# Graph-attention logits, masks and left sums on 32x32 tiles of TensorE, with the masks copied to all four row groups

## The chip, the cores and the metric

The kernel runs on one core of one Trainium2 chip. The metric is the device time of the whole program in microseconds (us); lower is better. The core has TensorE (PE), VectorE (DVE), ScalarE (ACT), GpSimd (POOL) and SyncE (SP, which here only issues transfers), and sixteen DMA engines that move data between its on-chip memory and DRAM.

## The reference

`x` has 4096 rows of 512 numbers, `adj` is a 4096 x 4096 matrix, mostly zero. Two layers follow each other, each on `h = relu(layernorm(x))` and each added to `x`:

```python
# layer 0: full attention with the adjacency added twice to the scores
a = q @ k.T / sqrt(512) + adj + adj
x = x + softmax(a) @ v

# layer 1: graph attention, 8 heads of 64
nX = standardized heads of h @ W            # per head: (nX - mean) / (std + eps), a_ln, b_ln
kg = at1 + at2.T                            # two numbers per node and head
kg = leaky_relu(kg, 0.2) * adj              # times the edge weight
mg = where(adj != 0, kg, -32768.0)
x  = x + elu(softmax(mg) @ nX + nX)
```

## The kernel before

**Layer 0** runs over 256 tiles: `ic`, eight chunks of 512 destinations, by `jt`, 32 blocks of 128 sources. A tile of `adj` is turned on VectorE so that sources lie on the partitions, scores are added to it (L734), the exponential is taken in place (L738), and the weighted values are summed on TensorE (L777). Along the way, `for_layer_1` makes two things out of each turned tile and stores them in DRAM: `ng`, bf16, zero on an edge and -2^60 elsewhere (L712, stored to `nT_d` by L715), and `gs`, the edge weight or a tiny number (L714, stored to `gT_d` by L716).

**Layer 1** begins with projections and ends with a software pipeline over 512 steps `STEPS[n] = (ic, hg, jt)`: eight chunks of 512 destinations, two groups of four heads, 32 blocks of 128 sources. The lines of a step:

- `load_adj(q)` loads four steps at once (JB = 4): `z2` (the sources' factors of the logits), the masks `nb` and `nx`, and the edge weights `g`. `nb` holds the masks on the partitions of their sources; `nx` holds the same rows with the two halves of 64 partitions exchanged. All go through SP's queue, two buffers each.
- `open_group(n, queue)` loads, once per group of 32 steps, `z1` (the destinations' factors), `u4`, and two six-row pieces of `z1_left`, whose other rows are zero.
- `sums(n)` makes the logits of four heads on TensorE: `z_product` (L1065), one matmul per head with six rows of the array at row group 32 x head, and then the masks: an identity times the mask, added to the logits (L1095), two heads at a time, four 64x64 tiles each. Two heads go to the left PSUM tile `l`, two to the right tiles `r`.
- `left_sums(n + 1)` (L1075) starts the next step's left tile with four 64x64 matmuls, and `left_relu` (L1081) takes 4 x relu of it on ScalarE in place; the logits are then added on top.
- `right_leaky` (L1113, VectorE) and `right_weigh` (L1119, GpSimd) finish the two right heads, `left_weigh` (L1122, VectorE) the two left ones. `exponent` (L1126, ScalarE) follows two steps later, `values` (L1134, TensorE, accumulated in `accs`) four steps later.

The program order on every engine is written out by hand and kept (`keep_in_program_order`, called `seq`); so are the places where loads are issued. In an iteration of the loop over `n` SP issues `load_adj(n // 4 + 1)` where `n` is a multiple of four, then what a group needs; TensorE does `sums(n)`, `left_sums(n + 1)` and `values(n - 4)`; `finish` and its tasks in `later` close a group. The projections' loop issues the first loads by `at_block(14, ...)`. Sources lie on the partitions as 4 column blocks of 32: P = 128, SB = 4, R = 32, HD = 64, GC = 512.

Of the kernel before, what the change touches and what calls it, by code (L numbers as in the profile page):

```python
# [11 lines left out]
BF16 = mybir.dt.bfloat16  # L12
# [6 lines left out]
P = 128  # L19
N = 4096  # L20
D = 512
NH = 8
HD = 64
NB = N // P
SB = 4
# [10 lines left out]
GC = 512  # L36
NI = N // GC
# [42 lines left out]
def fast_path(  # L80
# [18 lines left out]
    nc = tc.nc  # L99
    seq = tc.keep_in_program_order  # L100
# [3 lines left out]
    R = 32  # L104
# [10 lines left out]
    dram = ctx.enter_context(tc.tile_pool(name="dram", bufs=1, space=DRAM))  # L115
# [3 lines left out]
    ident_b = const.tile([P, P], BF16, name="ident_b")  # L119
# [25 lines left out]
    x1_d = dram.tile([NI, 2, P, SB, 2, P], F32, name="x1_d")  # L145

    gT_d = dram.tile([NB, P, N], F32, name="gT_d")
    nT_d = dram.tile([NB, P, N], BF16, name="nT_d")

# [1 line left out]
    z1_d = dram.tile([P, 2, N], BF16, name="z1_d")  # L153
# [172 lines left out]
    with tc.tile_pool(name="rows_in", bufs=2) as rows_in, tc.tile_pool(  # L326
        name="early", bufs=2
# [69 lines left out]
        with tc.tile_pool(name="proj_v", bufs=1) as pv, tc.tile_pool(  # L397
            name="proj_c", bufs=1
# [208 lines left out]
            for k in range(KC):  # L607
                pa = psum.tile([P, 512], F32, name="pa", tag="XZ"[k % 2], bufs=2)
                for c in range(SB):
                    seq(nc.tensor.matmul(  # L610
                        pa, turned["q"][:, c, ts(k, P)], turned["k"][:, c, :],
                        start=c == 0, stop=c == SB - 1,
# [71 lines left out]
        with tc.tile_pool(name="turns", bufs=6) as turns, tc.tile_pool(  # L684
            name="attn", bufs=2
# [22 lines left out]
            def for_layer_1(s):  # L708
                ic, jt = TILES[s]
                aT = turned[s] if s >= SB else firsts[s]  # L710
                ng = work.tile([P, GC], BF16, name="ng", tag="ng", bufs=2)
                seq(nc.vector.tensor_scalar(ng, aT, 0.0, NEG_BIG, ALU.is_equal, ALU.mult))  # L712
                gs = work.tile([P, GC], F32, name="gs", tag="gs", bufs=2)
                seq(nc.vector.scalar_tensor_tensor(gs, ng, G_MASKED / NEG_BIG, aT, ALU.mult, ALU.add))  # L714
                nc.sync.dma_start(out=nT_d[jt, :, ts(ic, GC)], in_=ng)  # L715
                nc.sync.dma_start(out=gT_d[jt, :, ts(ic, GC)], in_=gs)  # L716

            def product(out, s, name_a, name_b, start):
# [269 lines left out]
    with tc.tile_pool(name="ga_g", bufs=2) as adjs, tc.tile_pool(  # L988
        name="ga_in", bufs=2
    ) as inputs, tc.tile_pool(name="gat", bufs=1) as gat, tc.tile_pool(  # L990
        name="ga", bufs=2
# [7 lines left out]

        later = {}  # L1000

        z1_lefts = [gat.tile([P, GC], BF16, name=f"z1_left{k}") for k in range(2)]
        for z in z1_lefts:
            seq(nc.vector.memset(z, 0.0))

        def load_adj(q):
            ic, _, jt = STEPS[q * JB]
            z2 = inputs.tile([P, JB * P], BF16, name="z2", tag="z2", bufs=2)
            seq(nc.sync.dma_start(
                out=z2, in_=z2_d[:, STEPS[q * JB][1], jt * P : (jt + JB) * P]  # L1010
            ))
            ng = inputs.tile([P, JB, GC], BF16, name="nb", tag="nb", bufs=2)
            seq(nc.sync.dma_start(
                out=ng, in_=nT_d[jt : jt + JB, :, ts(ic, GC)].rearrange("t p i -> p t i")
            ))

            nx = inputs.tile([P, JB, GC], BF16, name="nx", tag="nx", bufs=2)
            for r in range(2):
                seq(nc.sync.dma_start(
                    out=nx[ts(r, HD)],  # L1020
                    in_=nT_d[jt : jt + JB, ts(1 - r, HD), ts(ic, GC)].rearrange("t p i -> p t i"),
                ))
            g = adjs.tile([P, JB, GC], F32, name="g", tag="g", bufs=2)
            seq(nc.sync.dma_start(
                out=g, in_=gT_d[jt : jt + JB, :, ts(ic, GC)].rearrange("t p i -> p t i")
            ))
            loads[q] = (g, (ng, nx), z2)

        def cols(ic, hg):
            rows = slice(ic * GC, (ic + 1) * GC)  # L1030
# [2 lines left out]
        def open_group(n, queue):  # L1033

            ic, hg, _ = STEPS[n]
            z1_left = z1_lefts[(2 * ic + hg) % 2]
            for first in (0, HD):
                rows = slice(first, first + 6)
                seq(queue.dma_start(out=z1_left[rows, :], in_=z1_d[rows, hg, ts(ic, GC)]))
            z1 = inputs.tile([P, GC], BF16, name="z1", tag="z1", bufs=2)  # L1040
            seq(queue.dma_start(out=z1, in_=z1_d[:, hg, ts(ic, GC)]))
            u4 = inputs.tile([P, 2, GC], F32, name="u4", tag="u4", bufs=2)
            groups[ic, hg] = {"z1": z1, "z1_left": z1_left, "u4": u4}
            load_u4(n, 0, queue)

        def load_u4(n, e, queue):
# [11 lines left out]

        lefts, rights = {}, {}

        def z_product(n, hh, out, start):

            ic, hg, jt = STEPS[n]
            rows = slice(32 * hh, 32 * hh + 6)
            seq(nc.tensor.matmul(  # L1065
                out, loads[n // JB][2][rows, ts(jt % JB, P)], groups[ic, hg]["z1"][rows, :],
                start=bool(start), stop=False, skip_group_check=not start,
            ))

        def left_sums(n):  # L1070

            lefts[n] = psum.tile([P, 2, GC], F32, name="l", tag="l", bufs=2)
            ic, hg, jt = STEPS[n]
            for r, c in ((0, 0), (1, 1), (0, 1), (1, 0)):
                seq(nc.tensor.matmul(  # L1075
                    lefts[n][ts(c, HD), r, :], loads[n // JB][2][ts(r, HD), jt % JB * P + c * HD :][:, :HD],
                    groups[ic, hg]["z1_left"][ts(r, HD), :], start=True, stop=True,
                ))

        def left_relu(n):  # L1080
            seq(nc.scalar.activation(lefts[n], lefts[n], AF.Relu, scale=4.0))  # L1081

        def sums(n):

            jt = STEPS[n][2]
            left = lefts[n]
            right = [psum.tile([P, GC], F32, name=f"r{e}", tag=f"r{e}", bufs=1) for e in range(2)]
            out = [left[:, 0, :], right[0], left[:, 1, :], right[1]]
            for hh in (1, 3, 0, 2):
                z_product(n, hh, out[hh], hh % 2)  # L1090
            masks = loads[n // JB][1]
            for first in (1, 0):
                for r, c in ((0, 0), (1, 1), (0, 1), (1, 0)):
                    rows = ts(r, HD)
                    seq(nc.tensor.matmul(  # L1095
                        out[first + 2 * r][ts(c, HD), :], ident_b[rows, rows],
                        masks[r != c][rows, jt % JB, :], start=False, stop=True,
                        skip_group_check=first == 0,
                    ))
            rights[n] = right  # L1100

        def both_heads(n):
# [361 lines left out]
        def at_block(r, f, *a):  # L1464
            at_blocks.setdefault(r, []).append(lambda: f(*a))
# [26 lines left out]
        at_block(0, rests[0])  # L1492
        at_block(12, first_group)
        at_block(14, load_adj, 0)
        for ic in range(2):
            load_normalized(ic)
        for r in range(-1, NB):
# [38 lines left out]
        for n in range(n_steps + 4):  # L1536

            q = n // JB + 1
            if n == n_steps:

                check_early()
                last_in.append(work.tile([P, HG, GC], F32, name="t", tag="t", bufs=6))
                for k, ap in enumerate((own_d[NI - 1, :, :, 1], x1_d[NI - 1, 1])):
                    seq(nc.sync.dma_start(
                        out=last_in[0][:, 2 * k : 2 * k + 2, :].rearrange("p f c -> p (f c)")
                        .rearrange("p (b d) -> p b d", b=SB),
                        in_=ap.rearrange("p b f d -> p b (f d)"),
                    ))
            if n % JB == 0 and q < n_steps // JB:
                load_adj(q)  # L1550
            if n + 10 < n_steps and STEPS[n + 10][2] == 0:
                open_group(n + 10, nc.sync)
            if n + 6 < n_steps and STEPS[n + 6][2] == 0:
                load_u4(n + 6, 1, nc.sync)
            if n < n_steps:
                sums(n)
            for f in left.pop(n, []):
                f()
            if n + 1 < n_steps:
                left_sums(n + 1)  # L1560
            if n < n_steps:
                right_leaky(n)
                right_weigh(n)
            if n + 1 < n_steps:
                left_relu(n + 1)
            done, ready = 0 <= n - 4 < n_steps, 0 <= n - 2 < n_steps
            if done and n < n_steps + 1:
                values(n - 4, 0)
            extra(n, "mid")
            if n < n_steps:  # L1570
                left_weigh(n)
            if done:
                if n < n_steps + 1:
                    values(n - 4, 1)
                if n % JB == 3:
                    loads.pop((n - 4) // JB)
            if n == n_steps + 3:
                for m, hf in ((n - 6, 0), (n - 5, 0), (n - 6, 1), (n - 5, 1)):
                    values(m, hf)
                for hf in range(2):  # L1580
                    values(n - 4, hf)
            if done and STEPS[n - 4][2] == NB - 1:
                if ready:
                    exponent(n - 2, slice(0, 2))
                finish(n, *STEPS[n - 4][:2])
                if ready:
                    exponent(n - 2, slice(2, 4))
            elif ready:
                exponent(n - 2)
            extra(n, "end")  # L1590
# [404 lines left out]
```

## Time and profile before

| what | value |
|---|---|
| median of 3 runs | 3541.22 us (3538.57 to 3542.74) |
| profiled execution: its own time | 3538.39 us |
| its span | 3536.6 us |
| mean granted TensorE clock | 0.996 |
| PE, DVE, ACT, POOL busy | 99%, 73%, 50%, 65% of the span |
| DMA | 779.07 MB, mean 220 GB/s |

The page divides the span into 40 slices and gives the busy share of each engine in each slice in tenths; layer 0 covers the first half and layer 1, whose loop begins near 1940 us, the second. The windows give the same by stretches of time. The chain of waits follows, from the last instruction back, what released each step. PEld is TensorE's loading of weights, which overlaps its matmuls; SPq is SP's queue of transfers.

### The profile page before, as it was taken

What the parts mean: (1) busy time and instruction counts of PE and PEld (TensorE: products, weight loads), DVE (VectorE), ACT (ScalarE), POOL (GpSimd) and SP (SyncE); (2) the same over time, 40 slices, a digit from 0 to 9 for tenths busy, and PEclk for the clock granted to TensorE, in tenths of its full rate; (3) what the DMA queues carried; (4) which work ended last, traced back from release to release, by engine and by line L of the source; (5) the groups of instructions that cost most, each with busy time, mean ns of one, the idle gap of its engine ahead of it and who ended that gap; (6) DMA issues with size and microseconds to landing.
All of it is one profiled execution on the core that took longest, in us unless ns stands there. A gap on an engine that the chain in (4) does not pass through costs nothing.

```text
span 3536.6 us, 59808 instructions
## 1 busy us (share of the span) xinstructions
PE 3492.0 (99%) x21898; PEld 2149.6 (61%) x21898; DVE 2574.3 (73%) x4262; ACT 1771.1 (50%) x1580; POOL 2285.6 (65%) x1863
## 2 busy tenths in 40 slices
PE   9999999999999999999999999999999999999998
PEld 7888888888888888888887223223222323232232
DVE  6765665656565666656567888888888888888887
ACT  2100111111111111111133999999999999999997
POOL 6754444444444444444567888788888888888886
PEclk9999999999999999999999999999999999999999
DMA  6688888888888888888768777787778877777885
GB/s 226 219 247 246 233 232 250 234 244 247 235 246 247 231 252 241 237 248 232 235 135 183 210 207 204 205 208 214 211 209 219 214 215 206 198 209 209 214 213 147
DMA packets 633550, 779.07 MB, mean 220 GB/s; under 512 B 78560, under 2 KB 461216, under 8 KB 624032
## 3 DMA queue, kind: packets, MB, share of 16 engines
q1 hardware_dynamic: 615680, 742.34, 73.5%
q0 software_dynamic: 16464, 31.98, 5.3%
q8 instruction: 174, 2.85, 0.3%
q10 hardware_dynamic: 1104, 0.85, 0.1%
q14 instruction: 128, 1.05, 0.1%
HBM read 592.97 MB, written 174.19 MB: 217 GB/s over the span
## 4 chain that ended last, share of the span: by engine, by line
PE 90%; DVE 7%; ACT 1%; DMA 1%; issue 1%; SPq 0%; DVEq 0%; ACTq 0%
PE accs L1134 25%; PE XZ L722 21%; PE M L777 20%; PE r L1095 4%; PE r L1065 4%; PE l L1075 3%; PE X L508 3%; PE l L1095 3%; PE Z L508 2%; DVE t L1122 2%; PE y L1327 1%; PE pt L1198 1%; DVE x L837 1%; DVE y L1211 1%; PE accs L1327 1%
## 5 line engine op out<-in xcount | busy, mean ns | idle before, releaser
L1119 POOL TENSOR_TENSOR t<-t,g 128x1024 f32<-128x1024 f32 x512 | 1225.6, 2406 | 268.9 <-DVE t L1113 233.3
L1134 PE MATMUL accs<-t,nX 128*64 128x512 f32 x4096 | 1003.0, 605 | 4.6 <-DVE ob L1188 4.6
L1126 ACT ACTIVATE t<-t 128x2048 f32<-128x2048 f32 (+1 forms) x527 | 976.5, 1853 | 0.2 <-POOL t L1119 0.2
L1113 DVE SCALAR_TENSOR_TENSOR t<-u,at2m,r 128x512 f32<-128x512 f32 x1024 | 719.3, 744 | 194.2 <-issue 152.0
L738 ACT ACTIVATE aT<-aT 128x512 f32<-128x512 f32 x256 | 161.2, 630 | 1387.3 <-DVE aT L734 1387.3
L734 DVE TENSOR_TENSOR aT<-aT,XZ 128x256 f32<-128x256 f32 x884 | 348.7, 418 | 575.1 <-PE XZ L722 570.8
L1122 DVE TENSOR_TENSOR t<-l,g 128x1024 f32<-128x1024 f32 x512 | 623.4, 1218 | 0.0
L1081 ACT ACTIVATE l<-l 128x1024 f32<-128x1024 f32 x512 | 516.3, 1008 | 117.5 <-PE l L1075 66.2
L1134 PEld LDWEIGHTS accs<-t,nX 128*64 128x64 f32 x4096 | 246.5, 136 | 461.9 <-issue 449.5
L722 PE MATMUL XZ<-qt,hS 128*128 128x256 f32 x2024 | 479.1, 379 | 1.0
L750 POOL TENSOR_TENSOR S<-aT 128x256 f32<-128x256 f32 x128 | 93.5, 731 | 506.9 <-ACT aT L738 506.9
L722 PEld LDWEIGHTS XZ<-qt,hS 128*128 128x128 f32 x2024 | 383.9, 190 | 55.9 <-DVE aT L734 4.0
L722 PE MATMUL XZ<-qt,hT 128*128 128x256 f32 x1520 | 369.5, 379 | 0.0
L762 POOL TENSOR_TENSOR total<-total,aT 128x256 f32<-128x256 f32 x360 | 323.0, 910 | 9.4
L722 PEld LDWEIGHTS XZ<-qt,hT 128*128 128x128 f32 x1520 | 288.8, 190 | 39.3
L1065 PEld LDWEIGHTS <-z 6*128 6x128 bf16 x2048 | 52.4, 91 | 422.2 <-DVE t L1113 353.8
L751 POOL TENSOR_TENSOR aT<-aT 128x256 f32<-128x256 f32 x128 | 93.6, 731 | 284.1 <-ACT aT L738 284.0
L777 PE MATMUL M<-tv,aT 128*128 128x256 f32 x1024 | 262.6, 379 | 0.0
L777 PE MATMUL M<-v,aT 128*128 128x256 f32 x1024 | 262.6, 379 | 0.0
L777 PE MATMUL M<-v,S 128*128 128x256 f32 x1024 | 242.5, 380 | 0.0
L714 DVE SCALAR_TENSOR_TENSOR gs<-ng,aT 128x512 f32<-128x512 bf16 x252 | 222.7, 884 | 8.7
L777 PEld LDWEIGHTS M<-v,aT 128*128 128x128 f32 x1024 | 194.6, 190 | 26.5
(267 smaller groups left out, 4552.4 us busy)
## 6 DMA issues: line engine op xcount, KB each, us to landing
g<-gT_d SPq DMA_DIRECT2D x128, 1024.0 KB
ag<-in_adj_dram SPq DMA_DIRECT2D x256, 256.0 KB
hS<-s_d SPq DMA_DIRECT2D x64, 1024.0 KB
gT_d<-gs SPq DMA_DIRECT2D x256, 256.0 KB
nb<-nT_d SPq DMA_DIRECT2D x128, 512.0 KB
nx<-nT_d SPq DMA_DIRECT2D x256, 256.0 KB
hT<-h_d SPq DMA_DIRECT2D x64, 768.0 KB
tv<-vt_d SPq DMA_DIRECT2D x128, 384.0 KB
```

The costliest lines, as they stand in the source:

```text
L714: seq(nc.vector.scalar_tensor_tensor(gs, ng, G_MASKED / NEG_BIG, aT, ALU.mult, ALU.add))
L722: seq(nc.tensor.matmul(out, a, b, start=start and k == 0, stop=k == 1, skip_group_check=not start,))
L734: seq(nc.vector.tensor_add(p, before, part))
L762: seq(nc.gpsimd.tensor_add(t, t, a))
L777: seq(nc.tensor.matmul(sums[ic][i][:, u, :], a[:, ts(u, P)], b, start=jt == 0 and u == 0, stop=jt == NB - 2, skip_group_check=u == 1,))
L1081: seq(nc.scalar.activation(lefts[n], lefts[n], AF.Relu, scale=4.0))
L1095: seq(nc.tensor.matmul(out[first + 2 * r][ts(c, HD), :], ident_b[rows, rows], masks[r != c][rows, jt % JB, :], start=False, stop=True, ski ...
L1113: seq(nc.vector.scalar_tensor_tensor(t[:, 2 + e, :], u4[:, e, :], at2m[:, jt, h : h + 1], right[e], ALU.max, ALU.add))
L1119: seq(nc.gpsimd.tensor_mul(t[:, 2:4, :], t[:, 2:4, :], both_heads(n)))
L1122: seq(nc.vector.tensor_mul(logits[n][:, 0:2, :], lefts.pop(n), both_heads(n)))
L1126: seq(nc.scalar.activation(t, t, AF.Exp))
L1134: seq(nc.tensor.matmul(accs[ts(e, HD), hf, :], nX[jt // SB][:, jt % SB, hg * HG + 2 * hf + e, :], t[:, hf + 2 * e, :], start=jt == 0, stop ...
```

## The change

`nT_d` gets a layout in which, for one tile, the four column blocks of 32 sources stand beside each other: 32 rows of 4 x 512. The store of `ng` is rearranged for it. `load_masks(n)` reads that block once per step and copies it to all four groups of 32 partitions, with a broadcast in front (four buffers, issued three steps ahead, ahead of `load_adj`); `nb` and `nx` and their loads are gone. So every row group of the array has all 128 sources' masks, 32 sources by 32 sources. `z_products` and the mask matmuls are written for 32x32 tiles, row group `hh` (the head) and column group `c` (the block of sources). `left_sums` uses `z_products` with `z1` itself, so `z1_left`, its loads and its memsets go.

```diff
--- before.py
+++ after.py
@@ -145,7 +145,7 @@
     x1_d = dram.tile([NI, 2, P, SB, 2, P], F32, name="x1_d")
 
     gT_d = dram.tile([NB, P, N], F32, name="gT_d")
-    nT_d = dram.tile([NB, P, N], BF16, name="nT_d")
+    nT_d = dram.tile([NB, NI, R, SB, GC], BF16, name="nT_d")
 
@@ -712,7 +712,7 @@
                 seq(nc.vector.tensor_scalar(ng, aT, 0.0, NEG_BIG, ALU.is_equal, ALU.mult))
                 gs = work.tile([P, GC], F32, name="gs", tag="gs", bufs=2)
                 seq(nc.vector.scalar_tensor_tensor(gs, ng, G_MASKED / NEG_BIG, aT, ALU.mult, ALU.add))
-                nc.sync.dma_start(out=nT_d[jt, :, ts(ic, GC)], in_=ng)
+                nc.sync.dma_start(out=nT_d[jt, ic].rearrange("p c i -> c p i"), in_=ng)
                 nc.sync.dma_start(out=gT_d[jt, :, ts(ic, GC)], in_=gs)
 
             def product(out, s, name_a, name_b, start):
@@ -999,32 +999,28 @@
 
         later = {}
 
-        z1_lefts = [gat.tile([P, GC], BF16, name=f"z1_left{k}") for k in range(2)]
-        for z in z1_lefts:
-            seq(nc.vector.memset(z, 0.0))
-
         def load_adj(q):
             ic, _, jt = STEPS[q * JB]
             z2 = inputs.tile([P, JB * P], BF16, name="z2", tag="z2", bufs=2)
             seq(nc.sync.dma_start(
                 out=z2, in_=z2_d[:, STEPS[q * JB][1], jt * P : (jt + JB) * P]
             ))
-            ng = inputs.tile([P, JB, GC], BF16, name="nb", tag="nb", bufs=2)
-            seq(nc.sync.dma_start(
-                out=ng, in_=nT_d[jt : jt + JB, :, ts(ic, GC)].rearrange("t p i -> p t i")
-            ))
-
-            nx = inputs.tile([P, JB, GC], BF16, name="nx", tag="nx", bufs=2)
-            for r in range(2):
-                seq(nc.sync.dma_start(
-                    out=nx[ts(r, HD)],
-                    in_=nT_d[jt : jt + JB, ts(1 - r, HD), ts(ic, GC)].rearrange("t p i -> p t i"),
-                ))
             g = adjs.tile([P, JB, GC], F32, name="g", tag="g", bufs=2)
             seq(nc.sync.dma_start(
                 out=g, in_=gT_d[jt : jt + JB, :, ts(ic, GC)].rearrange("t p i -> p t i")
             ))
-            loads[q] = (g, (ng, nx), z2)
+            loads[q] = (g, z2)
+
+        masks = {}
+
+        def load_masks(n):
+
+            ic, _, jt = STEPS[n]
+            masks[n] = inputs.tile([P, SB, GC], BF16, name="nb", tag="nb", bufs=4)
+            seq(nc.sync.dma_start(
+                out=masks[n].rearrange("p c i -> p (c i)"),
+                in_=nT_d[jt, ic].rearrange("p c i -> p (c i)").unsqueeze(0).to_broadcast([SB, R, SB * GC]),
+            ))
 
         def cols(ic, hg):
             rows = slice(ic * GC, (ic + 1) * GC)
@@ -1033,14 +1029,10 @@
         def open_group(n, queue):
 
             ic, hg, _ = STEPS[n]
-            z1_left = z1_lefts[(2 * ic + hg) % 2]
-            for first in (0, HD):
-                rows = slice(first, first + 6)
-                seq(queue.dma_start(out=z1_left[rows, :], in_=z1_d[rows, hg, ts(ic, GC)]))
             z1 = inputs.tile([P, GC], BF16, name="z1", tag="z1", bufs=2)
             seq(queue.dma_start(out=z1, in_=z1_d[:, hg, ts(ic, GC)]))
             u4 = inputs.tile([P, 2, GC], F32, name="u4", tag="u4", bufs=2)
-            groups[ic, hg] = {"z1": z1, "z1_left": z1_left, "u4": u4}
+            groups[ic, hg] = {"z1": z1, "u4": u4}
             load_u4(n, 0, queue)
 
         def load_u4(n, e, queue):
@@ -1058,45 +1050,42 @@
 
         lefts, rights = {}, {}
 
-        def z_product(n, hh, out, start):
+        def z_products(n, hh, out, **flags):
 
             ic, hg, jt = STEPS[n]
-            rows = slice(32 * hh, 32 * hh + 6)
-            seq(nc.tensor.matmul(
-                out, loads[n // JB][2][rows, ts(jt % JB, P)], groups[ic, hg]["z1"][rows, :],
-                start=bool(start), stop=False, skip_group_check=not start,
-            ))
+            rows = slice(R * hh, R * hh + 6)
+            for c in range(SB):
+                seq(nc.tensor.matmul(
+                    out[ts(c, R), :], loads[n // JB][1][rows, jt % JB * P + c * R :][:, :R],
+                    groups[ic, hg]["z1"][rows, :], **flags,
+                ))
 
         def left_sums(n):
 
             lefts[n] = psum.tile([P, 2, GC], F32, name="l", tag="l", bufs=2)
-            ic, hg, jt = STEPS[n]
-            for r, c in ((0, 0), (1, 1), (0, 1), (1, 0)):
-                seq(nc.tensor.matmul(
-                    lefts[n][ts(c, HD), r, :], loads[n // JB][2][ts(r, HD), jt % JB * P + c * HD :][:, :HD],
-                    groups[ic, hg]["z1_left"][ts(r, HD), :], start=True, stop=True,
-                ))
+            for r in range(2):
+                z_products(n, 2 * r, lefts[n][:, r, :], start=True, stop=True)
 
         def left_relu(n):
             seq(nc.scalar.activation(lefts[n], lefts[n], AF.Relu, scale=4.0))
 
         def sums(n):
 
-            jt = STEPS[n][2]
             left = lefts[n]
             right = [psum.tile([P, GC], F32, name=f"r{e}", tag=f"r{e}", bufs=1) for e in range(2)]
             out = [left[:, 0, :], right[0], left[:, 1, :], right[1]]
-            for hh in (1, 3, 0, 2):
-                z_product(n, hh, out[hh], hh % 2)
-            masks = loads[n // JB][1]
-            for first in (1, 0):
-                for r, c in ((0, 0), (1, 1), (0, 1), (1, 0)):
-                    rows = ts(r, HD)
+            order = (1, 3, 0, 2)
+            for hh in order:
+                right_one = hh % 2 == 1
+                z_products(n, hh, out[hh], start=right_one, stop=False, skip_group_check=not right_one)
+            for hh in order:
+                rows = ts(hh, R)
+                for c in range(SB):
                     seq(nc.tensor.matmul(
-                        out[first + 2 * r][ts(c, HD), :], ident_b[rows, rows],
-                        masks[r != c][rows, jt % JB, :], start=False, stop=True,
-                        skip_group_check=first == 0,
+                        out[hh][ts(c, R), :], ident_b[rows, rows], masks[n][rows, c, :],
+                        start=False, stop=True, skip_group_check=hh % 2 == 0,
                     ))
+            masks.pop(n)
             rights[n] = right
 
         def both_heads(n):
@@ -1492,6 +1481,8 @@
         at_block(0, rests[0])
         at_block(12, first_group)
         at_block(14, load_adj, 0)
+        for n in range(3):
+            at_block(14, load_masks, n)
         for ic in range(2):
             load_normalized(ic)
         for r in range(-1, NB):
@@ -1546,6 +1537,8 @@
                         .rearrange("p (b d) -> p b d", b=SB),
                         in_=ap.rearrange("p b f d -> p b (f d)"),
                     ))
+            if n + 3 < n_steps:
+                load_masks(n + 3)
             if n % JB == 0 and q < n_steps // JB:
                 load_adj(q)
             if n + 10 < n_steps and STEPS[n + 10][2] == 0:
```

## The prediction

> **What bounds the kernel now.** I read the page's busy times and slices first, then the windows of the two layers, then the chain of waits inside one layer-1 step, then the SP queue and the transfers, because the change touches matmuls and loads at once.
>
> ```profile
> PE 3492.0 (99%) x21898; PEld 2149.6 (61%) x21898; DVE 2574.3 (73%) x4262; ACT 1771.1 (50%) x1580; POOL 2285.6 (65%) x1863
> ...
> ACT  2100111111111111111133999999999999999997
> ...
> DMA  6688888888888888888768777787778877777885
> ```
>
> The second half (layer 1) has PE and ACT both at 9. The windows give shares:
>
> ```profile
> 335.00:2000.00 1665.00, 1651.75 (x7979) 1411.55 (x7981) 1047.67 (x2129) 301.80 (x455) 835.31 (x1034) 0.99 0.83 231
> 2040.00:3500.00 1460.00, 1447.41 (x11870) 435.00 (x11868) 1245.39 (x1559) 1355.93 (x995) 1198.14 (x550) 1.00 0.79 210
> ```
>
> Columns: window, length, busy PE, PEld, DVE, ACT, POOL, then clock, DMA share, GB/s. In layer 1 PE is busy 99%, ACT 1355.93/1460 = 93%, the sixteen DMA engines 79% on average. In layer 0 the DMA engines are at 83% beside a PE that never waits.
>
> The chain of waits through one step of layer 1 is TensorE alone:
>
> ```profile
> 2798.78 0.32 PE r L1065 x2
> 2799.11 0.01 PE l L1065 x2
> 2799.11 0.34 PE r L1095 x4
> 2799.45 0.22 PE l L1095 x4
> 2799.67 0.22 PE l L1075 x4
> 2799.89 1.87 PE accs L1134 x8
> 2801.75 0.32 PE r L1065 x2
> ```
>
> A step takes 2801.75 - 2798.78 = 2.97 us: 1.11 us of logits, masks and left sums, 1.87 us of values. So a step is PE's, ACT is next at 0.93 x 2.97 = 2.75 us, and loads hide. How four steps are loaded stands in the timeline of the SP queue:
>
> ```profile
> 2811.03 0.33 SPq L1009 DMA_DIRECT2D z<-z_d  x1
> 2811.57 0.36 SPq L1013 DMA_DIRECT2D nb<-nT_d  x1
> 2812.02 1.25 SPq L1019 DMA_DIRECT2D nx<-nT_d  x2
> 2815.43 0.36 SPq L1024 DMA_DIRECT2D g<-gT_d  x1
> ```
>
> The next four come 11.9 us later. And two windows show that equally busy DMA engines need not move equally much (last columns again: clock, share, GB/s):
>
> ```profile
> 2803.00:2805.00 2.00, 2.00 (x16) 0.41 (x12) 2.00 (x3) 2.00 (x2) 1.32 (x2) 1.00 0.98 192
> 2809.00:2810.50 1.50, 1.50 (x8) 0.29 (x4) 1.50 (x3) 1.50 (x2) 0.91 (x2) 1.00 1.06 356
> ```
>
> In the first mostly `nx` moves, in DMAs that write 64 partitions; in the second, rows for all 128. By the packet records a 1,024-byte row takes about 88 ns in the first and 46 ns in the second.
>
> **What the Trainium skill says.** "DMA: Bandwidth & Descriptors", section "Why a DMA increments its semaphore by 16 and not by 1": a DMA is split over the largest k up to 16 that divides the slowest dimension of both access patterns, and on SP's queue each of those k engines posts one +1. Its "Rules for kernel authors" add that a leading broadcast of c copies confines a DMA to at most c engines. The trace agrees with the rule: SP issued 2,232 DMAs, and its queue q1 has 35,392 four-byte packets, exactly 16 x 2,200 + 6 x 32; the 32 are the `z1_left` loads, which have six rows. "SBUF — State Buffer", section "Door 1: The DMA port swizzle": partitions 0-31 and 32-63 lie on the same eight of sixteen ports. The 88 ns against 46 agree. "TensorE: Matmul & The Clock Gate", Part 3: sixteen 32x32 tiles run together, starts some 4 ns apart. The trace shows it for four 64x64 tiles (3 to 4 ns apart); sixteen it doesn't show.
>
> **The change, part by part.**
>
> TensorE. Left sums go from 4 matmuls to 8, logits from 4 to 16, masks from 8 to 16: 16 become 40, with as many weight loads. If sixteen tiles overlap, the masks are one pack instead of two and save the 0.22 us of "l L1095"; logits and masks then use one tile size, which may save the 0.32 - 0.22 = 0.10 us that the logits take over a pack. 24 more starts at 4 ns cost 0.10 us. Net -0.2 us (bounds -0.3, and +1.1 if tiles of one row group went one after another: twice 0.88 and 0.44 against 1.11). -0.2 us is also all that ACT's 2.75 us lets through.
>
> The mask load. Its source is `unsqueeze(0).to_broadcast([SB, R, SB * GC])`: the slowest dimension is 4 (copies), the destination's is 128. By the rule k = 4: engine c carries the copy for partitions 32c to 32c+31, 32 rows of 4,096 bytes, every step. No row of before has such a packet on this queue; between the medians for 3,072 bytes (121 ns) and 8,192 bytes (309 ns) a straight line gives 158 ns, so 32 x 158 = 5.1 us per step on four engines (bounds 4.7, and 9.6 if each packet takes the 1.9-fold of the 64-partition rows). The same four also carry their sixteenth of the rest: `g`, 8 rows x 90 ns = 0.7; `z2`, 2 x 50 = 0.1; the accumulating transfers of POOL's queue, 9.2% of a 2.97 us step in the window 2400 to 3400, 0.27; `u4`, output, instruction fetches and semaphores about 0.1. That is 1.2 us. Against this, `nb` and `nx` go (1 MB per four steps over sixteen engines). I take 5.5 us for the masks, some packets meeting on a port, since engines drift: at 2812.0 one still brings `g` rows while others are in the next loads. Sum 5.5 + 1.2 = 6.7 us a step. Four mask buffers keep three transfers queued, so those engines never rest and their 6.7 us is the period; PE, ACT, DVE and POOL (2.97 us at most) hide beneath, with any gain or loss of TensorE below 3.7 us.
>
> SP's queue. Per four steps 6 DMAs instead of 5, at 0.33 to 0.36 us: 2.1 us of 27, free. load_masks(n+3) waits at the head for PE to finish the masks of step n-1; behind it stand `z2`, `g`, `u4` and the output. `g` follows up to four mask loads on the four rings and is needed four steps later; it lands with the last of them, so it adds its own 0.7 us, counted above. Two `z1_left` loads per group, two memsets and the first three mask loads (during the projections) lie off the path: 0.
>
> Layer 0. The store `nT_d[jt, ic].rearrange("p c i -> c p i")` also has a slowest dimension of 4. A tile of the loop takes (1785.3 - 241.7)/255 = 6.05 us between exponentials (L738); 0.83 of it is 5.0 us per engine. The store's 8 rows x 46 = 0.4 us become, on four engines, 32 x 46 to 32 x 88 = 1.5 to 2.8 us: 6.1 to 7.4 us against 6.05. PE loses 0 to 1.35 us per tile; waits at shared ports within the 0.83 ease when twelve engines are ahead, so I take 0.3 x 256 = 80 us (0 to 350; nothing here is on PE's path, so no gain).
>
> **Sum.** In the profiled execution (span 3536.6, its time 3538.4, 2.8 under the median of 3541.2) layer 1's loop runs from the first L1119 at 1941.2 to the last at 3513.9: 1572.7 us for 511 periods. The rest is 3538.4 - 1572.7 = 1965.7. After: 1965.7 + 80 + 512 x 6.7 (3430) = 5476; with the 2.8 us to the median 5480 us.
>
> **The rivals.**
>
> (a) Same confinement, ports shared throughout. Engines 0 and 1 walk partitions 0-31 and 32-63 in step, so every packet meets another on its port. For it: the 192 GB/s window. Against: a lag of four rows takes them apart. 9.6 + 1.2 = 10.8 us a step: 1966 + 150 + 5530 = 7650. In between lies everything from 5500 up.
>
> (b) Faster: the mask load spreads over sixteen engines, so that the four-fold copy is cheap. Then an engine has 8 x 158 ns = 1.3 us plus 1.2 us, 2.5 us in a 2.97 us step, and stays hidden; TensorE's -0.2 us shows: 3541 - 512 x 0.2 = 3440. It decides wherever the load falls below 2.75 us per step, which needs about ten engines or more. Against it: the count of 35,392, and the broadcast as the slowest dimension in the diff.
>
> (c) Sixteen engines, but tiles of a row group serialize: +1.1 us x 512 gives 4100, slower.
>
> That the change does not do what it says: it does load four row groups, but "broadcast" is the very thing that costs.
>
> **How the numbers follow.** Forecast 0.58, (a) with the stretch below it 0.34, (b) 0.05, (c) 0.03. Slower 0.94; faster 0.05; within 0.2% (about what a measurement of this kernel can tell from no change) 0.01. Forecast's low end: masks 4.7, others 1.1, layer 0 at 0: 5.8 x 512 + 1969 = 4940, rounded to 5050 because both lows at once are unlikely; the top is (a), 7650. That leaves out (b), (c) and a sliver of either end.
>
> **What would show it.** Right: a layer-1 step near 6.7 us (L1119 starts), PE at roughly half, waiting at the mask matmuls for `nb`; ACT near 40%; mean DMA share far below 0.79 in layer 1 while the time grows; packets of 4,096 bytes near 158 ns, about 260 ns or more for (a); k = 4 in the count of four-byte packets. The forecast is wrong if PE stays at 99%, or the share stays near 0.8: then the load was spread. Layer 0 is wrong if its loop keeps 6.05 us or exceeds 7.4.

## The result and the profile after

| | before | after |
|---|---|---|
| median | 3540.36 us (6 runs) | 5490.61 us (5482.04 to 5500.56, 6 runs) |
| ratio | 1 | 1.5513, 95% interval 1.5496 to 1.553 |
| span of the profiled execution | 3536.6 us | 5490.3 us |
| layer 0, from one exponential to the next (L738) | 6.05 us | 6.11 us |
| layer 1, mean step (first to last right weighing: L1119 before, L1108 after) | 3.08 us | 6.85 us |

The kernel is slower by 1950 us, nearly all of it in layer 1: its 511 steps took 3500.3 us in place of 1572.7. The loop starts 26.6 us later (1967.8 against 1941.2), of which layer 0 makes 14 us.

The page of the changed kernel, busy times and slices:

```profile
PE 4161.6 (76%) x34186; PEld 2238.2 (41%) x34186; DVE 2585.6 (47%) x4260; ACT 1778.1 (32%) x1580; POOL 2268.7 (41%) x1863
...
PE   9999999999999866665666666666666666666566
...
DMA  6788889888888654444444444444444444444443
GB/s 220 244 224 243 235 247 240 236 243 235 242 242 230 153 137 134 133 132 133 133 131 134 130 135 133 133 136 128 131 137 129 135 132 133 135 130 134 135 128 112
```

Read the DMA row against the time. In layer 1 the mean share of sixteen engines fell from 7 or 8 tenths to 4, and the bytes per second fell too, while the kernel grew longer. A mean of 0.4 looks like spare capacity; it is four engines without a pause and twelve mostly idle. The records of single packets show it: from 2100 to 5300 us four of the 4,096-byte packets that the mask load consists of are under way at once in 54% of the time, three or fewer in 40%, and five or six in 6% (records of successive packets can overlap). Packets of any kind are fewer than four at once in 1% of the time. The windows say the same (busy PE, PEld, DVE, ACT, POOL, then clock, share, GB/s):

```profile
335.00:2000.00 1665.00, 1620.58 (x7845) 1401.59 (x7843) 1019.95 (x2090) 263.57 (x424) 795.59 (x1016) 0.99 0.85 227
2100.00:5300.00 3200.00, 2031.05 (x22822) 510.95 (x22823) 1228.44 (x1530) 1337.08 (x976) 1164.73 (x536) 0.71 0.44 133
```

Four full engines of sixteen are 0.25. The rest of 0.44 is what the other loads take on the twelve others. The chain of waits through layer 1, which was TensorE alone, is now the mask load:

```profile
3953.96 23.50 DMA nb<-nT_d
3977.46 0.04 issue
3977.50 0.62 PE r L1084 x8
3978.13 0.03 PE l L1084 x8
3978.16 0.43 PE l L1058 x8
3978.59 1.17 PE accs L1123 x3
3979.76 24.55 DMA nb<-nT_d
```

One load takes 23 to 25 us from issue to the end. That is three and a half steps of 6.85 us: up to four loads stand in line for the same four engines. The engines' waits (engine, line, what it waited for: us in total, times, longest):

```profile
ACT l L1070 <- PE l L1058: 2024.8, 511, 9.2
...
PE r L1084 <- DMA nb<-nT_d: 1269.7, 422, 8.7
```

TensorE waits at the mask matmuls (L1084) for `nb`, and ScalarE, behind it in the order, for the next left sums.

The count of four-byte packets confirms the split. SP issued 2,328 DMAs, of which 768 have a slowest dimension of 4 (512 mask loads, 256 stores): 16 x 1,560 + 4 x 768 = 28,032, and the queue q1 has 28,032 such packets.

### The profile page after: what moved, and what is told of

Its sections match the earlier page's. It is cut to its first block, busy times and chain, and to the rows that moved or that the text cites. A ratio compares the mean times of both kernels' runs of the same rounds, so it can differ in the third digit from the quotient of the medians.

```text
span 5490.3 us, 84578 instructions
## 1 busy us (share of the span) xinstructions
PE 4161.6 (76%) x34186; PEld 2238.2 (41%) x34186; DVE 2585.6 (47%) x4260; ACT 1778.1 (32%) x1580; POOL 2268.7 (41%) x1863
## 4 chain that ended last, share of the span: by engine, by line
DMA 61%; PE 35%; DVE 2%; SPq 2%; issue 1%; ACT 0%; POOL 0%; DVEq 0%; ACTq 0%; POOLq 0%
DMA nb<-nT_d 54%; PE XZ L722 12%; PE M L777 11%; PE accs L1123 3%; DMA z<-z_d 3%; DMA tv<-vt_d 3%; PE X L508 2%; PE Z L508 2%; PE r L1084 1%; PE y L1316 1%; PE l L1058 1%; SPq L1020 1%; DMA gT_d<-gs 1%; PE accs L1316 1%; DVE aT L734 0%
## 5 line engine op out<-in xcount | busy, mean ns | idle before, releaser
L1108 POOL TENSOR_TENSOR t<-t,g 128x1024 f32<-128x1024 f32 x512 | 1206.3, 2356 | 2217.9 <-DVE t L1102 1902.5
L1123 PE MATMUL accs<-t,nX 128*64 128x512 f32 x4096 | 1545.7, 891 | 0.0
L1084 PE MATMUL r<-nb,ident_b 32*32 32x512 bf16 x4096 | 276.6, 514 | 1271.6 <-DMA nb<-nT_d 1269.7
L1084 PEld LDWEIGHTS <-ident_b 32*32 32x32 bf16 x8192 | 118.5, 93 | 1440.6 <-issue 1440.4
L1123 PEld LDWEIGHTS accs<-t,nX 128*64 128x64 f32 x4096 | 339.6, 188 | 762.5 <-issue 762.4
L738 ACT ACTIVATE aT<-aT 128x512 f32<-128x512 f32 x256 | 161.2, 630 | 1401.9 <-DVE aT L734 1401.9
L1058 PE MATMUL l<-z,z 6*32 6x512 bf16 x8192 | 527.1, 490 | 6.8 <-DMA z<-z_d 4.6
L1058 PEld LDWEIGHTS <-z 6*32 6x32 bf16 x12288 | 136.5, 91 | 690.7 <-issue 426.0
L1084 PE MATMUL l<-nb,ident_b 32*32 32x512 bf16 x4096 | 276.8, 516 | 0.0
```

Source lines behind the costliest of these rows:

```text
L1058: seq(nc.tensor.matmul(out[ts(c, R), :], loads[n // JB][1][rows, jt % JB * P + c * R :][:, :R], groups[ic, hg]["z1"][rows, :], **flags,))
L1084: seq(nc.tensor.matmul(out[hh][ts(c, R), :], ident_b[rows, rows], masks[n][rows, c, :], start=False, stop=True, skip_group_check=hh % 2 == ...
L1108: seq(nc.gpsimd.tensor_mul(t[:, 2:4, :], t[:, 2:4, :], both_heads(n)))
L1123: seq(nc.tensor.matmul(accs[ts(e, HD), hf, :], nX[jt // SB][:, jt % SB, hg * HG + 2 * hf + e, :], t[:, hf + 2 * e, :], start=jt == 0, stop ...
```

## The experiments

**Four loads in place of one broadcast.** Same bytes, same packets, same TensorE work; only the slowest dimension changes from 4 to 32.

```diff
-            seq(nc.sync.dma_start(
-                out=masks[n].rearrange("p c i -> p (c i)"),
-                in_=nT_d[jt, ic].rearrange("p c i -> p (c i)").unsqueeze(0).to_broadcast([SB, R, SB * GC]),
-            ))
+            for c in range(SB):
+                seq(nc.sync.dma_start(
+                    out=masks[n][ts(c, R)].rearrange("p c i -> p (c i)"),
+                    in_=nT_d[jt, ic].rearrange("p c i -> p (c i)"),
+                ))
```

> The changed kernel with each step's mask load as four loads of 32 rows, one per row group, in place of one load with the broadcast in front; bytes, packets and TensorE's work are the same. Theory (the broadcast's slowest dimension of 4 confines the load to four engines): each load now runs on sixteen engines, but its 32 partitions reach eight ports, so 524 KB at the 192 GB/s of the 64-partition loads of before take 2.7 us, plus 1.2 us for the rest: 3.9 us a step, about 3980 us in all, the four-byte packets up to 16 per load. Rival (twice the mask bytes are too many for the memory): the step stays at 6.85 us, about 5490 us. Rival (the 40 small matmuls at a lowered clock are the bound): also about 5490 us.

Measured: 3891.03 us, ratio to before 1.0992 (1.0974 to 1.101), a little better than I gave; a step takes 3.74 us, a 4,096-byte packet 259 ns in the mean (181 in the changed kernel). The queue has 58,752 four-byte packets, 16 x 1,560 + 4 x 256 + 16 x 2,048: each of the 2,048 loads ran on sixteen engines. The window of layer 1:

```profile
2100.00:3500.00 1400.00, 1216.32 (x18408) 369.34 (x18409) 986.24 (x1235) 1071.34 (x787) 946.02 (x437) 0.91 0.96 245
```

The share is 0.96: now all sixteen engines are full. Of the 1950 us, spreading the load over them brought back 1600 us. Both rivals (too many bytes, TensorE) are refuted as the main cause. That the remaining 350 us come from engines that meet at the eight ports of 32 partitions is argued from the packet time. The next run writes 128 partitions in one load.

**The same load from 128 different rows.**

```diff
+            first = ic // SB * SB
             seq(nc.sync.dma_start(
                 out=masks[n].rearrange("p c i -> p (c i)"),
-                in_=nT_d[jt, ic].rearrange("p c i -> p (c i)").unsqueeze(0).to_broadcast([SB, R, SB * GC]),
+                in_=nT_d[jt, first : first + SB].rearrange("a p c i -> (a p) (c i)"),
             ))
```

> The changed kernel with a mask load of the same size and packet length whose source is 128 different rows (four neighbouring chunks of destinations, so the masks are those of other destinations). Slowest dimension 128 on both sides: sixteen engines and all ports. Theory: masks 1.3 to 1.5 us plus 1.2 us per engine and step, hidden; what is left is TensorE's own gain or loss. I expect -0.2 us a step against before, about 3440 us (3400 to 3560). If 32x32 tiles of one row group went one after another it would be about 4100 us. Rival (mask bytes are too many): 5490 us.

Measured: 3579.03 us, ratio 1.0113 (1.0096 to 1.0129). The same bytes, with packets back at 159 ns in the median, now cost 38 us against before (82 us against the run without mask traffic below), so they are not too many. But my 3440 us were a miss, and so was the range from 3400 up to 3560. This run changes three things against the four loads: the partitions of one load, the rows that are read (128 different ones in place of 32 read four times) and the number of loads. So it does not show alone that the ports are the reason of the 350 us. The 64-partition `nx` loads of before speak for the ports: each reads different rows, and their packets were slow too. The window:

```profile
2040.00:3450.00 1410.00, 1314.09 (x22058) 426.17 (x22052) 1179.89 (x1477) 1273.42 (x944) 1133.29 (x521) 0.97 0.87 291
```

PE is busy 93% in place of 99%, the DMA share is 0.87 at 291 GB/s. Undisturbed steps take 2.8 us, the mean is 3.12 us. The run with kept masks and the one with a deeper queue show where the gain went.

**Two broadcasts of two.** The suspected cost doubled, the bytes kept.

```diff
-            seq(nc.sync.dma_start(
-                out=masks[n].rearrange("p c i -> p (c i)"),
-                in_=nT_d[jt, ic].rearrange("p c i -> p (c i)").unsqueeze(0).to_broadcast([SB, R, SB * GC]),
-            ))
+            for c in range(2):
+                seq(nc.sync.dma_start(
+                    out=masks[n][ts(c, HD)].rearrange("p c i -> p (c i)"),
+                    in_=nT_d[jt, ic].rearrange("p c i -> p (c i)").unsqueeze(0).to_broadcast([2, R, SB * GC]),
+                ))
```

> The changed kernel with each step's mask load as two loads, each a broadcast of two copies (64 partitions); same bytes and packets. Theory[...]: both loads fall on the same two engines, 64 packets x 162 to 182 ns = 10.4 to 11.6 us plus 1.2 us: 11.6 to 12.8 us a step, 7900 to 8540 us in all. Rival (each load takes its own pair of engines): four engines as before, near 5490 us. Rival (bytes or TensorE): 5490 us.

Measured: 7949.97 us (one run), 11.62 us a step, packets of 168 ns in the mean: 64 x 168 ns = 10.8 us, and 0.8 left over. The window of layer 1:

```profile
2100.00:3500.00 1400.00, 671.60 (x5873) 154.51 (x5873) 314.70 (x388) 346.24 (x255) 297.55 (x135) 0.60 0.24 78
```

The share halves to 0.24. Two loads of two copies do not take four engines between them: both fall on the same pair. The packet records agree: from 2100 to 3500 us two 4,096-byte packets are under way at once in 83% of the time, three in 4%, and never four. With steps of 11.62 us on two engines, 6.85 on four and 3.74 on sixteen, the cause of the main loss is settled.

**Layer 0's store, in two forms.** First as four stores of 32 rows, then in plain row order.

```diff
-                nc.sync.dma_start(out=nT_d[jt, ic].rearrange("p c i -> c p i"), in_=ng)
+                for c in range(SB):
+                    nc.sync.dma_start(out=nT_d[jt, ic][:, c, :], in_=ng[ts(c, R)])
```

> The changed kernel with layer 0's store of the masks as four stores of 32 rows (slowest dimension 32, sixteen engines) in place of one with a slowest dimension of 4. Theory: a tile of layer 0 goes from 6.11 back to 6.05 us, -14 us in all, about 5475 us; layer 1 keeps 6.85 us. Rival (four more transfers per tile on SP's queue cost as much as they save): layer 0 stays at 6.11 us or above.

Measured: 5487.29 us (one run), 6.10 us per tile of layer 0. Spreading the store over sixteen engines did not help: a miss.

```diff
-                nc.sync.dma_start(out=nT_d[jt, ic].rearrange("p c i -> c p i"), in_=ng)
+                nc.sync.dma_start(out=nT_d[jt, ic].rearrange("p c i -> (p c) i"), in_=ng)
```

> The changed kernel with layer 0's store of the masks in plain row order (128 rows on sixteen engines and all ports; the order of the sources in the masks is then not the one that layer 1 takes them for). If the rearranged store causes layer 0's 0.06 us more per tile, its tile goes from 6.11 to 6.05 us; if it stays at 6.11, the store is not the cause. Layer 1 keeps about 6.85 us a step; in all 5475 to 5490 us.

Measured: 5473.65 us (one run), 6.05 us per tile, as before. A tile takes 6.11 to 6.13 us in all six runs of this document that have the rearranged store in one piece, and 6.05 in the three with rows in plain order. So the rearranged store is the cause of layer 0's 14 us, in either form. The waits in layer 0 of the changed kernel, 335 to 1790 us,

```profile
PEld M L777 <- issue: 14.8, 26, 1.5
PE M L777 <- DMA tv<-vt_d: 5.4, 11, 1.1
```

and of this run

```profile
PEld M L777 <- issue: 0.6, 2, 0.5
```

show where the time goes: TensorE stands before the weighted values. 5.4 us of it are named as waits for `tv`, which arrives late. Why four stores of 32 rows delay it as much (eight ports, or four more transfers in front of `tv`) these runs do not tell.

**TensorE's part alone.** The masks of the first four steps are kept and used throughout.

```diff
-            masks[n] = inputs.tile([P, SB, GC], BF16, name="nb", tag="nb", bufs=4)
-            seq(nc.sync.dma_start(
...
+            if n < 4:
+                kept.append(inputs.tile([P, SB, GC], BF16, name=f"nb{n}", tag=f"nb{n}", bufs=1))
+                seq(nc.sync.dma_start(
...
+            masks[n] = kept[n % 4]
```

> The changed kernel with the masks of the first four steps kept and used in all steps (mask loads left out after these, so the masks are those of other tiles). TensorE's work is the same 40 small matmuls a step; no mask traffic in layer 1. Theory (TensorE's part alone saves 0.2 us a step, as its undisturbed steps of 2.77 to 2.80 us show in the run with 128 different rows, and that run's loss against before is bursts of transfers): mean step about 0.15 to 0.2 us under that of before (3.08 us from first to last L1119 there), 3440 to 3490 us in all. Rival (the 40 matmuls bring other waits, with POOL and ACT): 3540 us or above.

Measured: 3496.67 us, ratio 0.988 (0.9863 to 0.9896); mean step 2.94 us, 0.14 below before. The total is just above the 3490 I gave, because the loop starts 30 us later (1971.4 against 1941.2; about half of it is layer 0). The chain of waits of one step:

```profile
2801.81 0.34 PE r L1060 x8
2802.14 0.03 PE l L1060 x8
2802.17 0.19 PE r L1086 x8
2802.36 0.03 PE l L1086 x8
2802.39 0.35 PE l L1060 x8
2802.74 1.87 PE accs L1125 x8
2804.61 0.34 PE r L1060 x8
```

Logits, masks and left sums take 0.94 us in place of 1.11: sixteen mask matmuls pass in one pack of 0.22 us and start 2 to 5 ns apart. So sixteen 32x32 tiles do overlap, and the change's own idea works. Without any mask traffic it is worth 1.2%.

The left sums, the 0.35, took 0.22 before. VectorE holds them up:

```profile
2801.07 1.22 DVE L1113 TENSOR_TENSOR t<-l,g 128x1024 f32<-128x1024 f32 x1
...
2801.97 0.40 PE L1086 MATMUL r<-nb,ident_b 32*32 32x512 bf16 x8
...
2802.34 0.41 PE L1060 MATMUL l<-z,z 6*32 6x512 bf16 x8
```

`left_weigh` (L1113) reads the left tile of an earlier step and ends at 2802.29; the left sums, which need one of the two buffers, start 0.05 us later. From 2400 to 2800 us they start within 0.08 us of its end in 128 of 137 steps; in the kernel before, in 18 of 130. So of what TensorE saves, about 0.13 us a step is lost again to VectorE.

**Logits and left sums alone on 32x32 tiles**, masks as before.

```diff
-            seq(nc.tensor.matmul(
-                out, loads[n // JB][2][rows, ts(jt % JB, P)], groups[ic, hg]["z1"][rows, :],
...
+            for c in range(SB):
+                seq(nc.tensor.matmul(
+                    out[ts(c, R), :], loads[n // JB][2][rows, jt % JB * P + c * R :][:, :R],
...
+            for r in range(2):
+                z_products(n, 2 * r, lefts[n][:, r, :], start=True, stop=True)
```

> The kernel before with the logits and left sums alone on 32x32 tiles; masks, their loads and their 64x64 tiles as before. Theory: packs of matmuls stay as many as before (logits, two of masks, left sums), the switch from 32x32 to 64x64 tiles stays and one more comes before the left sums; 16 more matmuls start 4 ns apart, 0.06 us a step. 3540 to 3600 us. Rival (the smaller tiles themselves are faster): under 3530 us.

Measured: 3608.86 us, ratio 1.0195 (1.0178 to 1.0212), a little above what I gave. The chain of one step:

```profile
2799.84 0.34 PE r L1066 x8
2800.18 0.03 PE l L1066 x8
2800.21 0.34 PE r L1092 x4
2800.55 0.22 PE l L1092 x4
2800.76 0.34 PE l L1066 x8
2801.10 1.87 PE accs L1131 x8
```

Logits, masks and left sums take 0.34 + 0.03 + 0.34 + 0.22 + 0.34 = 1.27 us against 1.11; the left sums, the last 0.34, took 0.22 before, after masks of their own tile size. Small tiles without the mask's part are a loss. The extra 0.12 us fits a change of tile size, of which this version has one more: before, too, the masks cost 0.34 us after logits of another tile size and 0.22 us after masks of their own.

**128 rows with a deeper queue.** Five buffers instead of four, loads issued four steps ahead instead of three, on top of the run with 128 different rows.

```diff
-            masks[n] = inputs.tile([P, SB, GC], BF16, name="nb", tag="nb", bufs=4)
+            masks[n] = inputs.tile([P, SB, GC], BF16, name="nb", tag="nb", bufs=5)
...
-            if n + 3 < n_steps:
-                load_masks(n + 3)
+            if n + 4 < n_steps:
+                load_masks(n + 4)
```

> The kernel with 128 different rows as the source of the mask load (masks of other destinations), with five mask buffers and loads issued four steps ahead in place of four and three. If its waits for masks are bursts that a deeper queue takes up, the mean step falls from 3.12 towards 2.9 us, 3470 to 3540 us in all; if the sixteen engines are simply too busy (share 0.87), it stays at 3580 us.

Measured: 3524.52 us (one run), mean step 3.01 us. One more buffer and the earlier issue gave back 55 us of the 82 us between the run with 128 rows and the run without mask traffic: that speaks for bursts as the larger part; the share is still 0.89.

Only two of these kernels ran faster than before: the one that leaves out the mask loads, and this one, which loads the masks of other destinations. So no version here that brings every step its own masks is faster than before. One was not tried: layer 0 could store each block four times, so that a load has 128 rows of its own, at four times the bytes of that store.

## Why the prediction was right

The forecast was 5480 us; measured were 5490.61. The mechanism is the one that was forecast; that the total is so close is luck. The loop took 3500 us against 3430 forecast, and layer 0 cost 14 us in place of 80, so two misses of about 70 us cancel. By its steps:

- **The mask load on four engines**: right. A 4,096-byte packet was put at 158 ns, with 5.5 us a step for some meetings at ports. Measured: median 162, mean 181 ns, so 32 x 181 = 5.8 us. The text said that before had no such packet on SP's queue. That was wrong: there are 128, at the very end, with a median of 159 ns, and they would have given the same price without the straight line. (The line itself started from 121 ns for 3,072 bytes; the median over the whole run is 124.)
- **The rest on the same engines**: put at 1.2 us. The remainder is 6.85 - 5.8 = 1.05 us, but that is no measurement of the rest: by the packet records, everything but the mask packets takes 1.56 us a step of an average engine. `g` alone is larger than forecast, 8 rows of 128 ns in place of 90. 5.8 + 1.56 is 7.4, above the 6.85 that a step takes, so the durations of packets can't simply be added. The sum of 6.7 came out near for this reason too.
- **Ports shared throughout, rival (a)**: wrong for this load. It needed about 300 ns a packet; the upper tenth begins at 256. In the four loads of 32 rows the mean is 259 ns. Longer packets fit engines that meet at a port sometimes in the one case and mostly in the other; where each engine writes is not in the record, and why the pair would drift apart was not tested. The 88 ns behind the factor 1.9 hold for the first half of the window shown; over all of it the mean is 81 ns.
- **TensorE's -0.2 us**: right within what was hidden: 0.94 us against 1.11 for the logits, masks and left sums. Rival (c), tiles that go one after another, is refuted. But rival (b)'s 3440 us was too good: even with no mask traffic the time is 3497 us. 0.2 us in every step was too much: an ordinary step gained 0.17, and the mean step 0.14, since five of the 32 steps of a group, in which the group before is closed, take 3.7 us in both kernels and got no shorter. The later start of the loop, 30 us, is the other part. The limit behind TensorE was named wrongly, too: in the run with kept masks not ScalarE's 2.75 us but VectorE's `left_weigh` holds up the next left sums.
- **How many engines (b) needs**: "about ten" was a slip. By the prediction's own prices, 128 x 158 ns = 20.2 us of packets have to fit into 2.75 - 1.2 = 1.55 us, which takes thirteen.
- **Layer 0**: right in kind, too large: +80 us forecast, 14 us measured. A tile ended at the low end of the 6.1 to 7.4 us; why so little of the store's longer time is felt was not tested.
- **The first three mask loads, put at 0**: a small miss. From layer 0's last exponential to the first L1108 168 us pass, 156 before. It is 156 to 160 us in the runs whose mask loads run on sixteen engines from the start and 183 us with two engines, so these loads on four engines are late.
- **SP's queue**: as said, it sets nothing. It waits at the mask loads (L1020) for buffers that TensorE frees late, 848.8 us in total behind `accs`.
- **What the text said would show it**: PE was put at roughly half in layer 1 and is at 63%, because the clock fell (0.71) and the same work looked longer; ACT is at 42%.

## What to carry to other kernels

Before a load is written as a broadcast, look at the slowest dimension of both its sides. In these runs a small number there, 2 or 4, was the number of DMA engines, and two such loads shared the same few; four plain loads brought back 1600 of 1950 us. In a profile, a low mean DMA share with one load at the end of the chain is the sign of this. Last, price an idea that needs more copies of its data by the copies first: here the matmuls could win 1.2% at the most, and the best tried way of bringing the copies, four plain loads, costs 9.9%.

## What the hardware showed beyond that

- The granted TensorE clock was lower the longer TensorE waited: 1.00 in layer 1 before, 0.91 with steps of 3.74 us, 0.71 at 6.85 us, 0.60 at 11.62 us. These are means: the clock records of the changed kernel know only 1.0 and 0.5, in stretches of 3.4 us and more, and 60% of the time from 2100 to 3400 us is at 0.5. The values of a step then take up to 3.4 us in place of 1.87; here this hides under the load.
- A change of tile size on TensorE costs about 0.1 us: from the first matmul of a pack of 512 columns to the first of the next, 0.22 to 0.25 us pass where both have one tile size, and 0.31 to 0.36 us where they differ (kernel before and the two runs on TensorE's part, at a clock of 1.00). The left sums that wait for VectorE are not counted here.
